# Four selective-scan layers on one core: the engines take the scans' instructions in the order of the source

## The chip, the cores and the metric

The kernel runs on one core of a Trainium2 chip. A core has a matrix engine (TensorE, PE), a vector engine (VectorE, DVE), an engine for activation functions (ScalarE, ACT), a general-purpose engine (GpSimd, POOL) and an engine that here only issues transfers (SyncE, SP). Each has its own queue of instructions and they meet through semaphores. The metric is the device time of one execution in microseconds; lower is better.

## What is computed

Four layers are applied one after the other to 8 images of 48 x 48 positions and 96 channels, each as x + layer(groupnorm(x)). A layer projects 96 channels to 2 x 192, convolves one half with a 3 x 3 window for each channel, and runs a recurrence over the 2,304 positions in four directions (by rows, by columns, and both backwards) with 16 states for each of the 192 channels. Layers 0 to 2, cut to what matters:

```python
delta = softplus(dts + bias)                    # per position and channel
def step(h, inp):
    u, dl, Bv, Cv = inp
    dA = exp(dl[..., None] * A)                 # A: 16 states per channel
    h = h * dA + (dl * u)[..., None] * Bv[:, :, None, :]
    y = einsum('bkdn,bkn->bkd', h, Cv)          # sum over the 16 states
    return (h, y)
# four directions are summed, then layernorm, times silu(z), projection to 96
```

The last layer computes h from cumulative sums in place of the recurrence; its decay makes all but the ends of the sequences vanish, and the kernel computes only those (with a full version behind a test that it makes at run time).

## The kernel before

The images go in 4 pairs; 192 channels times two images fill three tiles of 128 partitions. For each of 3 layers, 4 pairs, 3 tiles, 2 phases (rows, columns), 2 directions and 3 chunks of 768 positions there are 16 states, so 6,912 units of work. One unit, with the engine of each instruction:

```python
def pooled(self, n):                # every fourth state has dB u made on GpSimd
    return n % 4 == 3 and self.l < NLAYER - 1

def weigh(self, n):                 # POOL: bb = B (broadcast by DMA) * (delta u)
    if self.pooled(n):
        b = self.b[n][:, : self.m]
        nc.gpsimd.tensor_mul(b, b, self.du)

def exp(self, n, da):               # ACT: exp(delta A)
    ...
def spread(self, n):                # pooled: ACT puts exp(delta A) into PSUM
    ...                             # else:   PE spreads the row B over 128 partitions
    for z, zm in pieces(self.m):    #         into a PSUM tile b (two of them)
        nc.tensor.matmul(b[:, z : z + zm], w, self.brow[:k, z : z + zm], ...)

def scan(self, n):
    ...
    if not self.pooled(n):
        nc.vector.tensor_mul(b, self.du, b)                         # DVE: dB u
    h = b if self.pooled(n) else da
    nc.vector.tensor_tensor_scan(way(h), way(da), way(b), start, ALU.mult, ALU.add)
    ...
    if not self.last:
        nc.scalar.copy(carries[:, n : n + 1], h[:, end : end + 1])  # ACT: carry
    nc.gpsimd.tensor_mul(c, c, h)                                   # POOL: C h

def add_up(self, n):                # PE: sum over the states, identity matmuls
    ...
    if n == NS - 1:
        self.collect()              # DVE: y += acc
```

The loop that writes these out runs ahead for what is needed later, and weaves three generators in: `coming` (softplus of the next chunk), `behind` (the epilogue of the last pair: layernorm, gate, projection) and `ahead` (the prologue of the next pair: group norm, projections, convolution, and `split`, which cuts B and C into three bf16 parts), the last from two thirds of a pair on:

```python
LAG = 4
LOADS, DECAYS = 3, 2
...
for k, ((l, p, unit), c, n) in enumerate(todo):
    ...                             # at unit == after (2/3): ahead = begin(*following)
    get_ready(k + 1)                # loads of k + 4, spread of k + 1, weigh and exp of k + 3
    c.scan(n)
    step(coming)
    if unit >= after:
        step(ahead, 8 if l in short else 1)
    elif l in short:
        step(behind, 6)
    elif unit % 2 == 0:
        step(behind)
    if k >= LAG:
        b.add_up(n)                 # of unit k - 4
        ...
```

`short` holds the last layer. The program is written as straight code, and the compiler's scheduler decides in which order each engine takes its instructions, as long as the data allow it. Tiles come from pools with a fixed number of buffers: 9 for C (`cb`), 3 for B on GpSimd (`bb`), 5 for exp(delta A) (`da`), 2 PSUM tiles for `b`, 2 PSUM banks for everything else, 1 for the sum.

Of the kernel before, what the change touches and what calls it, by code (L numbers as in the profile page):

```python
# [35 lines left out]
BF16 = mybir.dt.bfloat16  # L39
AF = mybir.ActivationFunctionType  # L40
ALU = mybir.AluOpType

P = 128
NB, H, W, DM = 8, 48, 48, 96
# [31 lines left out]
def nx(rank):  # L76

    return 2 * rank + 4 * NS
# [17 lines left out]
def ss2d_layers_kernel(ctx: ExitStack, tc: tile.TileContext, x_in, consts, weights, out):  # L96
    nc = tc.nc
# [48 lines left out]
    for b in range(2):  # L146
# [3 lines left out]
            mybir.AxisListType.X,  # L150
            ALU.add,
        )
# [7 lines left out]
    nc.vector.tensor_reduce(  # L160
        mine, ident.rearrange("p (b q) -> p b q", b=2), mybir.AxisListType.X, ALU.add
    )
# [4 lines left out]
    class Layer:  # L167


        def __init__(self, l):  # L170
            self.l = l
            self.rank = r = RANKS[l]
            self.nx = nx(r)
            cols, n = weight_columns(r)
            wt = wpool.tile([P, n], F32, name=f"w_{l}", tag="w")
            nc.sync.dma_start(wt, weights[l])
            part = {k: wt[:, a:b] for k, (a, b) in cols.items()}
            self.inw = part["inw"][0:DM]
            self.xp = part["xp"].rearrange("p (t f m) -> p t f m", t=2, f=2)
            self.dtw = part["dtw"].rearrange("p (k d) -> p k d", k=4)  # L180
            self.outw = part["outw"].rearrange("p (t c) -> p t c", t=2)
            self.outw_2 = wpool.tile([P, 2, DM], F32, name=f"outw2_{l}", tag="outw2")
            for b in range(2):
                nc.vector.tensor_scalar_mul(
                    self.outw_2[:, b, :], self.outw[:, 1, :], mine[:, b : b + 1]
                )
            self.par = part["par"].rearrange("p (t c) -> p t c", t=2)

            self.a = wpool.tile([P, 2, 4 * NS], F32, name=f"a_{l}", tag="a")
            nc.scalar.activation(self.a, self.par[:, :, C_ALOG : C_ALOG + 4 * NS], AF.Exp)  # L190
            nc.vector.tensor_scalar_mul(self.a, self.a, -1.0)

            self.amax = wpool.tile([P, 2, 4], F32, name=f"amax_{l}", tag="amax")
            nc.vector.tensor_reduce(
                self.amax, self.a.rearrange("p t (k n) -> p t k n", n=NS),
                mybir.AxisListType.X, ALU.max,
            )
            self.dsum = wpool.tile([P, 2], F32, name=f"dsum_{l}", tag="dsum")
            nc.vector.tensor_reduce(
                self.dsum, self.par[:, :, C_D : C_D + 4], mybir.AxisListType.X, ALU.add  # L200
            )
            self.diag = None

        def make_diag(self):

            self.diag = dpool.tile([P, 2, 9, P], F32, name=f"diag_{self.l}", tag="diag")
            for t in range(2):
                for j in range(9):
                    nc.vector.tensor_scalar_mul(
                        self.diag[:, t, j, :], ident, self.par[:, t, C_CONVW + j : C_CONVW + j + 1]  # L210
                    )

        def column(self, t, c):
            return self.par[:, int(t == 2), c : c + 1]
# [22 lines left out]

    def prologue(l, p, short=False):
        ly = layers[l]
        if ly.diag is None:  # L240
            ly.make_diag()
        gn = sm2.tile([DM, 2, 2], F32, name=f"gn_{l}_{p}", tag="gn")
        xd = dram.tile([2, 2, ly.nx, L], F32, name=f"xd_{l}_{p}", tag=f"xd{ly.rank}")
        xb = dram.tile([2, 2, PARTS, 3 * NS, L], BF16, name=f"xb_{l}_{p}", tag="xb")
# [4 lines left out]
        def padded(name):  # L249
            pad = tmp.tile([P, H + 2, W + 2], F32, name=name, tag="tmp")  # L250
            nc.gpsimd.memset(pad[:, 0 : H + 2 : H + 1, :], 0.0)
            nc.gpsimd.memset(pad[:, 1 : H + 1, 0 : W + 2 : W + 1], 0.0)
            return pad
# [20 lines left out]
        def split(xt, c0, m, to):  # L274
# [13 lines left out]
                )  # L288
            yield

        pad2 = padded(f"pad2_{l}_{p}")
        for b in range(2):
            x = tmp.tile([DM, L], F32, name=f"x_{l}_{p}_{b}", tag="tmp")
# [43 lines left out]
            nc.scalar.activation(scale, scale, AF.Exp, scale=-0.5)  # L337
            nc.vector.scalar_tensor_tensor(shift, mg, -1.0, scale, ALU.mult, ALU.mult)
            yield
# [83 lines left out]
    def prepare(c):  # L423
# [16 lines left out]
        for z in range(0, c.m, HALF):  # L440
# [28 lines left out]
            yield  # L469
            nc.vector.scalar_tensor_tensor(v, v, 0.0, lg, ALU.max, ALU.add)  # L470
            yield
# [24 lines left out]
    def picked(t, n):  # L496
# [2 lines left out]
            return 2 * NR, pick2[:, n, :]  # L499
        return NR, pick[:, n : n + 1].to_broadcast([NR, P])  # L500

    class Chunk:


# [90 lines left out]
        def scan(self, n):  # L595
            m = self.m
            way = (lambda z: z) if self.d == 0 else (lambda z: z[:, ::-1])
            carries = self.group["carry"]
            start = 0.0 if self.first else carries[:, n : n + 1]
            da, c = self.da.pop(n), self.cb[n][:, :m]  # L600
            b = self.b.pop(n)[:, :m]
            if not self.pooled(n):
                nc.vector.tensor_mul(b, self.du, b)  # L603
            if self.l < NLAYER - 1:

                h = b if self.pooled(n) else da
                nc.vector.tensor_tensor_scan(way(h), way(da), way(b), start, ALU.mult, ALU.add)  # L607
            else:

                h = self.rq.pop(n)  # L610
                nc.vector.tensor_mul(b, h, b)
                nc.vector.tensor_tensor_scan(
                    way(h), ones.to_broadcast([P, m]), way(b), start, ALU.mult, ALU.add
                )
                nc.gpsimd.tensor_mul(c, c, da)
            if not self.last:
                end = m - 1 if self.d == 0 else 0
                nc.scalar.copy(carries[:, n : n + 1], h[:, end : end + 1])  # L618
            nc.gpsimd.tensor_mul(c, c, h)  # L619

        def add_up(self, n):
            if n == 0:
                self.acc = pacc.tile([P, 2 * BANK], F32, name="acc", tag="acc")
            c = self.cb.pop(n)
            for z, zm in pieces(self.m):
                nc.tensor.matmul(  # L626
                    self.acc[:, z : z + zm], ident, c[:, z : z + zm],
                    start=(n == 0), stop=(n == NS - 1),
                )
            if n == NS - 1:  # L630
                self.collect()

        def collect(self):

# [23 lines left out]
    class Edge:  # L658
# [82 lines left out]
        def add_up(self, i):  # L741
            if i == 0:
                self.acc = pacc.tile([P, 2 * BANK], F32, name="acc", tag="acc")
            c = self.cb.pop(i)
            for j in range(QUAD):
                nc.tensor.matmul(  # L746
                    self.acc[:, :EDGE], ident, c[:, j, :],
                    start=(i == j == 0), stop=(QUAD * i + j == NS - 1),
                )
            if QUAD * i + QUAD == NS:  # L750
                self.collect()

        def collect(self):
            l, p, t, s = self.l, self.p, self.t, state[self.l, self.p]
# [118 lines left out]
    def drain(g):  # L873
        for _ in g:
            pass

    def step(g, n=1):
        for _ in range(n):
            if next(g, StopIteration) is StopIteration:
                return  # L880

    groups = [(t, ph, d) for t in range(3) for ph in range(2) for d in range(2)]
    LAG = 4
    LOADS, DECAYS = 3, 2

    def run(pairs, short):
# [44 lines left out]
        drain(prepare(chunks[0]))  # L931
        coming_to = iter(chunks[1:])
        behind = ahead = coming = iter(())
        get_ready(0)
        for k, ((l, p, unit), c, n) in enumerate(todo):
            at = pairs.index((l, p))
            following = pairs[at + 1] if at + 1 < len(pairs) else None
            per = NS // QUAD if l in short else NS
            all_units = len(groups) * (per if l in short else len(SCANS) * per)

            after = 2 * all_units // 3
            if unit == after:
                drain(behind)
                if following:
                    ahead = begin(*following)
            if n == 0:
                drain(coming)
                if unit + per == all_units:
                    drain(ahead)
                coming = next(coming_to, None)  # L950
                coming = prepare(coming) if coming else iter(())
            if n == max(0, per - 1 - DECAYS):
                drain(coming)
            get_ready(k + 1)
            c.scan(n)
            step(coming)
            if unit >= after:
# [6 lines that stand above are left out]
                (bl, bp, _), b, n = todo[k - LAG]  # L964
                b.add_up(n)
                if todo[k - LAG + 1][0][:2] != (bl, bp):
                    behind = epilogue(bl, bp)
        for _, c, n in todo[-LAG:]:
            c.add_up(n)
        drain(epilogue(*pairs[-1]))  # L970

    last = NLAYER - 1
    run([(l, p) for l in range(NLAYER) for p in range(NPAIR)], (last,))


    every = sm1.tile([P, 1], F32, name="every", tag="every")
# [102 lines left out]
```

## Time and profile before

| | before |
|---|---|
| time, median of 3 runs | 25,929.62 us (25,909.55 to 25,961.06) |
| span of the profiled run | 25,950.1 us |
| mean granted TensorE clock | 0.855 of full |
| busy PE / PE loads | 20,502.7 / 9,651.0 us |
| busy DVE | 19,436.9 us |
| busy POOL | 18,407.7 us |
| busy ACT | 13,651.9 us |
| read and written | 3,650.53 and 164.07 MB, 147 GB/s |

The profile is that of one execution. "Busy" is the time in which an engine had an instruction in work[...]. A group of instructions is given as line, engine, operation, output and inputs, shapes and count, then its busy time and the mean of one, then the idle time of the engine just before them and what ended most of it. A wait is given as "engine tile line <- engine tile line", with its sum, its count and the longest. "issue" is idle time that no event of the profile explains. In the tables by stretches there are, for each engine, busy us and the number of instructions.

### The profile page before, as it was taken

To read this page: it belongs to the slowest core of one execution; us is meant where nothing else is said; L and a number is where in the kernel's file an instruction comes from. 1 tells how busy PE (TensorE), PEld (TensorE's weight loads), DVE (VectorE), ACT (ScalarE), POOL (GpSimd) and SP (SyncE) were. 2 spreads that over 40 slices of the span, in tenths; PEclk is the share of its full clock that TensorE was granted. 3 is DMA by queue.
4 is the path that set the end of the run, shared out by engine and by line. 5 is a ranking of instruction groups with operands and counts; after the bars stand their busy time and mean duration, and the time that the engine had idled before them with its cause. 6 is when DMAs were issued, how large, how long until landed. Compare 5 with 4: busy or idle time off the path is not lost. (4 is left out here: it accounts for less than half of the span.)

```text
span 25950.1 us, 229568 instructions
## 1 busy us (share of the span) xinstructions
PE 20502.7 (79%) x61890; PEld 9651.0 (37%) x61890; DVE 19436.9 (75%) x17126; ACT 13651.9 (53%) x23819; POOL 18407.7 (71%) x11561
## 2 busy tenths in 40 slices
PE   7787887887887887887887887887887887886886
PEld 2333333333433333333333433433433433334555
DVE  5867877876877877877877877877877877876443
ACT  4454554554554554554554554554554554555665
POOL 5767867867877867877877877877877877875332
PEclk8888888887888988898888897898898898897876
DMA  3545545545555555555555555545555555554121
GB/s 115 162 138 155 176 139 154 174 142 148 176 147 154 177 145 153 174 150 153 174 146 152 176 148 150 175 143 153 177 147 152 175 148 152 175 151 111 56 63 49
DMA packets 1714313, 3830.25 MB, mean 148 GB/s; under 512 B 224112, under 2 KB 588016, under 8 KB 1699824
## 3 DMA queue, kind: packets, MB, share of 16 engines
q1 hardware_dynamic: 1713008, 3815.46, 49.5%
q8 instruction: 500, 8.19, 0.1%
q14 instruction: 805, 6.59, 0.1%
HBM read 3650.53 MB, written 164.07 MB: 147 GB/s over the span
## 5 line engine op out<-in xcount | busy, mean ns | idle before, releaser
L626 PE MATMUL acc<-cb,cst 128*128 128x512 f32 (+1 forms) x27648 | 12436.5, 582 | 2350.2 <-POOL cb L619 1995.9
L619 POOL TENSOR_TENSOR cb<-cb,da 128x768 f32<-128x768 f32 x5184 | 9348.1, 1812 | 3056.7 <-DVE da L607 984.5
L626 PEld LDWEIGHTS acc<-cb,cst 128*128 128x128 f32 x27648 | 5543.0, 220 | 7898.7 <-issue 4396.8
L574 ACT ACTIVATE da<-dl,a 128x768 f32<-128x768 f32 x5184 | 4828.0, 933 | 5735.9 <-POOL cb L619 5703.7
L603 DVE TENSOR_TENSOR b<-du,b 128x768 f32<-128x768 f32 x5184 | 4871.6, 952 | 2871.6 <-PE b L591 2855.7
L607 DVE TENSOR_TENSOR_SCAN da<-da,carry,b 128x768 f32<-128x768 f32 x3456 | 6173.1, 1803 | 61.3 <-ACT da L574 3.5
L591 PE MATMUL b<-brow,pick 48*128 48x512 bf16 (+3 forms) x10368 | 2904.3, 366 | 2249.7 <-DVE da L607 1594.6
L546 POOL TENSOR_TENSOR bb<-bb,du 128x768 f32<-128x768 f32 x1728 | 3133.8, 1814 | 664.8 <-DMA bb<-xd 385.0
L619 POOL TENSOR_TENSOR cb<-cb,bb 128x768 f32<-128x768 f32 x1728 | 3135.8, 1815 | 594.8 <-issue 197.3
L607 DVE TENSOR_TENSOR_SCAN da<-da,b 128x768 f32<-128x768 f32 x1728 | 2983.4, 1743 | 28.4 <-ACT da L574 1.0
L607 DVE TENSOR_TENSOR_SCAN bb<-b,carry,bb 128x768 f32<-128x768 f32 x1152 | 2073.8, 1800 | 770.5 <-POOL bb L546 609.1
L591 PEld LDWEIGHTS <-pick 48*128 48x128 bf16 (+1 forms) x10368 | 758.7, 100 | 5014.5 <-DVE da L607 2729.1
L574 ACT ACTIVATE b<-dl,a 128x768 f32<-128x768 f32 x1728 | 1550.4, 897 | 654.5 <-DVE da L607 553.0
L618 ACT COPY carry<-da 128x1 f32<-128x1 f32 x3456 | 638.5, 185 | 2353.3 <-DVE da L607 2299.0
L262 PE MATMUL ps<-pad,diag 128*128 128x480 f32 (+1 forms) x4320 | 1801.6, 562 | 77.6 <-ACT u L227 48.2
L467 POOL TENSOR_TENSOR lg<-lg,w 128x384 f32<-128x384 f32 (+1 forms) x912 | 892.1, 978 | 1029.4 <-ACT w L465 847.5
L470 DVE SCALAR_TENSOR_TENSOR ps<-ps,lg 128x384 f32<-128x384 f32 (+1 forms) x912 | 499.8, 548 | 1127.0 <-POOL lg L468 1088.8
L607 DVE TENSOR_TENSOR_SCAN bb<-b,bb 128x768 f32<-128x768 f32 x576 | 1002.8, 1741 | 360.2 <-POOL bb L546 241.0
L262 PEld LDWEIGHTS ps<-pad,diag 128*128 128x128 f32 x4320 | 800.7, 193 | 884.6 <-issue 674.3
L450 PE MATMUL ps<-dts,w 6*128 6x384 f32 (+5 forms) x2432 | 946.6, 560 | 60.3 <-DVE ex L852 14.5
L468 POOL TENSOR_TENSOR lg<-lg,e 128x384 f32<-128x384 f32 (+1 forms) x912 | 889.9, 976 | 46.6
L791 PE MATMUL ps<-ey,cst 128*128 128x144 f32 (+1 forms) x4096 | 815.8, 345 | 120.4 <-ACT ey L815 104.0
(124 smaller groups left out, 17609.9 us busy)
## 6 DMA issues: line engine op xcount, KB each, us to landing
cb<-xd SPq DMA_DIRECT2D x4736, 384.0 KB
cb<-xd SPq DMA_DIRECT2D x4736, 192.0 KB
bb<-xd SPq DMA_DIRECT2D x1152, 384.0 KB
bb<-xd SPq DMA_DIRECT2D x1152, 192.0 KB
yd<-y SPq DMA_DIRECT2D x48, 1152.0 KB
ey<-yd SPq DMA_DIRECT2D x256, 216.0 KB
brow<-xb SPq DMA_DIRECT2D x576, 72.0 KB
xb<-parts SPq DMA_DIRECT2D x288, 108.0 KB
```

The lines of the kernel that those rows point to most:

```text
L262: nc.tensor.matmul(ps[:, :m], ly.diag[:, int(t == 2), j, :], pad[:, r0 + dy : r0 + dy + nr, dx : dx + W], start=(j == 0), stop=(j == 8),)
L450: nc.tensor.matmul(o[:, :m], ly.dtw[q0 : q0 + r, k, chans], dts[q0 : q0 + r, at], start=True, stop=True,)
L467: nc.gpsimd.tensor_sub(lg, lg, w1)
L468: nc.gpsimd.tensor_add(lg, lg, e)
L546: nc.gpsimd.tensor_mul(b, b, self.du)
L574: nc.scalar.activation(da, self.dl, AF.Exp, scale=columns_of(self.l, self.t, self.ph, self.d, n))
L591: nc.tensor.matmul(b[:, z : z + zm], w, self.brow[:k, z : z + zm], start=True, stop=True)
L603: nc.vector.tensor_mul(b, self.du, b)
L607: nc.vector.tensor_tensor_scan(way(h), way(da), way(b), start, ALU.mult, ALU.add)
L619: nc.gpsimd.tensor_mul(c, c, h)
L626: nc.tensor.matmul(self.acc[:, z : z + zm], ident, c[:, z : z + zm], start=(n == 0), stop=(n == NS - 1),)
L791: nc.tensor.matmul(o, mean_w[:, cols], z[:, b, :], start=True, stop=False)
```

## The change

The change makes each engine take the instructions of layers 0 to 2 in the order in which the source writes them. For that it draws an edge, which costs no semaphore, from every instruction to the previous one on the same engine, for the compiler's scheduler to respect. So that the written order is a fit one, it moves three things in the source: the copy of the carry and `collect` go into lists that the loop empties one unit later, just before the next scan; the product C h is written ahead of the carry copy; and the set-up of a layer (its derived weights and the diagonal matrices of the convolution) becomes steps of the prologue. Layer 3 isn't in the ordered stretch.

```diff
+    late_act, late_dve = [], []
+
+    def catch_up():
+        while late_dve:
+            late_dve.pop(0)()
+        while late_act:
+            nc.scalar.copy(*late_act.pop(0))
...
+            nc.gpsimd.tensor_mul(c, c, h)
             if not self.last:
                 end = m - 1 if self.d == 0 else 0
-                nc.scalar.copy(carries[:, n : n + 1], h[:, end : end + 1])
-            nc.gpsimd.tensor_mul(c, c, h)
+                late_act.append((carries[:, n : n + 1], h[:, end : end + 1]))
...
             if n == NS - 1:
-                self.collect()
+                late_dve.append(self.collect)
...
+    def mark():
+        marks.append(len(tc._region_blocks()[0].instructions))
+
+    def keep_order(a, b):
+        last = {}
+        info = mybir.DependencyInfo(mybir.DependencyClass.NoSync, mybir.DependencyReason.DATA)
+        for i in tc._region_blocks()[0].instructions[a:b]:
+            if i.engine in ENGINES:
+                if i.engine in last:
+                    tc.add_manual_dep(i, last[i.engine], info, reason="order")
+                last[i.engine] = i.name
...
         behind = ahead = coming = iter(())
+        mark()
         get_ready(0)
         for k, ((l, p, unit), c, n) in enumerate(todo):
...
+            if l in short and unit == 0:
+                mark()
...
             get_ready(k + 1)
+            catch_up()
             c.scan(n)
...
     run([(l, p) for l in range(NLAYER) for p in range(NPAIR)], (last,))
+
+    keep_order(*marks[:2])
```

In the layer's class (cut), what `__init__` and `make_diag` did at once becomes a generator that the prologue runs before its group norm:

```diff
+        def derive(self):
...
+            yield
...
-        def make_diag(self):
...
                     nc.vector.tensor_scalar_mul(
                         self.diag[:, t, j, :], ident, self.par[:, t, C_CONVW + j : C_CONVW + j + 1]
                     )
+                    if j % 3 == 2:
+                        yield
...
-        if ly.diag is None:
-            ly.make_diag()
...
+        if ly.diag is None:
+            for _ in range(4):
+                yield
+            yield from ly.derive()
```

More of the change, by code (lines that the diff above doesn't have):

```diff
@@ L41 @@
 ALU = mybir.AluOpType
+ENGINES = (
+    mybir.EngineType.PE, mybir.EngineType.DVE, mybir.EngineType.Activation,
+    mybir.EngineType.Pool, mybir.EngineType.SP,
+)
 P = 128
@@ L181, in __init__ @@
             self.outw = part["outw"].rearrange("p (t c) -> p t c", t=2)
+            self.par = part["par"].rearrange("p (t c) -> p t c", t=2)
+            self.diag = None
+        def derive(self):
+            l = self.l
             self.outw_2 = wpool.tile([P, 2, DM], F32, name=f"outw2_{l}", tag="outw2")
@@ L186, in __init__ @@
                 )
-            self.par = part["par"].rearrange("p (t c) -> p t c", t=2)
+            yield
             self.a = wpool.tile([P, 2, 4 * NS], F32, name=f"a_{l}", tag="a")
             nc.scalar.activation(self.a, self.par[:, :, C_ALOG : C_ALOG + 4 * NS], AF.Exp)
+            yield
             nc.vector.tensor_scalar_mul(self.a, self.a, -1.0)
@@ L201, in __init__ @@
             )
-            self.diag = None
-        def make_diag(self):
             self.diag = dpool.tile([P, 2, 9, P], F32, name=f"diag_{self.l}", tag="diag")
@@ L289, in split @@
             yield
+        if ly.diag is None:
+            for _ in range(4):
+                yield
+            yield from ly.derive()
         pad2 = padded(f"pad2_{l}_{p}")
@@ L750, in add_up @@
             if QUAD * i + QUAD == NS:
-                self.collect()
+                late_dve.append(self.collect)
         def collect(self):
@@ L880, in step @@
                 return
+    marks = []
+    def mark():
[8 more added lines that the diff above has]
+                last[i.engine] = i.name
     groups = [(t, ph, d) for t in range(3) for ph in range(2) for d in range(2)]
@@ L969, in run @@
             c.add_up(n)
+            catch_up()
         drain(epilogue(*pairs[-1]))
```

## The prediction

> **What bounds the kernel now.** I read the page first. No engine is full, and three are about equally far from it:
>
> ```profile
> PE 20502.7 (79%) x61890; PEld 9651.0 (37%) x61890; DVE 19436.9 (75%) x17126; ACT 13651.9 (53%) x23819; POOL 18407.7 (71%) x11561
> ...
> L619 POOL TENSOR_TENSOR cb<-cb,da 128x768 f32<-128x768 f32 x5184 | 9348.1, 1812 | 3056.7 <-DVE da L607 984.5
> L603 DVE TENSOR_TENSOR b<-du,b 128x768 f32<-128x768 f32 x5184 | 4871.6, 952 | 2871.6 <-PE b L591 2855.7
> L607 DVE TENSOR_TENSOR_SCAN da<-da,carry,b 128x768 f32<-128x768 f32 x3456 | 6173.1, 1803 | 61.3 <-ACT da L574 3.5
> L546 POOL TENSOR_TENSOR bb<-bb,du 128x768 f32<-128x768 f32 x1728 | 3133.8, 1814 | 664.8 <-DMA bb<-xd 385.0
> ```
>
> A unit of work here is one state of one chunk of 768 positions; layers 0 to 2 have 6,912 of them (5,184 + 1,728 scans), and DVE does one scan for each. The chain that ended last is useless here: it covers only the last 1% of the span. So I cut the span by time. The scans of layers 0 to 2 run from about 250 to 23,705 us, 1,955 us for each of 12 image pairs, and layer 3 takes the last 2,245 us. Within one pair the busy times by stretches of 100 us (columns: PE, PEld, DVE, ACT, POOL, then the granted clock, DMA share and GB/s) are very uneven:
>
> ```profile
> 10400.00:10500.00 100.00, 83.30 (x290) 40.92 (x288) 92.45 (x81) 58.80 (x102) 85.02 (x52) 0.90 0.59 183
> 11400.00:11500.00 100.00, 88.69 (x261) 40.96 (x260) 70.91 (x61) 57.16 (x83) 62.25 (x37) 0.98 0.47 135
> 11800.00:11900.00 100.00, 60.68 (x142) 26.13 (x142) 51.87 (x40) 34.39 (x55) 67.30 (x47) 0.78 0.53 141
> ```
>
> The first line is the **long part** of a pair (384 units, scans beside the epilogue of the previous pair): 10,200 to 11,200 us has 333 scans, 3.00 us per unit, with DVE 87.8% busy. The second is the convolution of the next pair's prologue, bound by PE. The third is the prologue's end (splitting B into three bf16 parts): nobody is above 70%, and 20 scans were done instead of 35. That is pure waiting. A pair is 384 x 3.00 = 1,152 us plus 803 us for the **prologue part** (192 units, 4.18 us each).
>
> The order in which the engines take their work explains much of that waiting. The timeline just at 10,000 us:
>
> ```profile
> 10001.28 1.81 POOL L619 TENSOR_TENSOR cb<-cb,bb 128x768 f32<-128x768 f32 x1 [1.35 <-issue]
> 10003.04 3.58 POOL L619 TENSOR_TENSOR cb<-cb,da 128x768 f32<-128x768 f32 x2
> ...
> 10006.57 1.82 POOL L546 TENSOR_TENSOR bb<-bb,du 128x768 f32<-128x768 f32 x1
> ...
> 10008.43 1.76 DVE L607 TENSOR_TENSOR_SCAN bb<-b,bb 128x768 f32<-128x768 f32 x1 [7.28 <-POOL bb L546]
> ...
> 10021.44 2.90 PE L626 MATMUL acc<-cb,cst 128*128 128x512 f32 x4 [3.35 <-POOL cb L619]
> ```
>
> POOL makes three products c h that nobody needs yet, while DVE stands 7.28 us for the product dB u behind them. The list of waits has these items, summed over the run:
>
> ```profile
> DVE b L603 <- PE b L591: 2855.7, 1796, 18.3
> DVE ps L470 <- POOL lg L468: 1088.8, 443, 161.6
> POOL rest L280 <- ACT parts L279: 894.5, 259, 116.1
> DVE bb L607 <- POOL bb L546: 850.1, 137, 15.1
> ```
>
> DVE's three lines are 4,795 us. Its idle time up to 23,000 us is 5,034 us (busy 17,966 us by the same table in coarser cuts), so they are nearly all of it.
>
> [...] DVE does nothing in those 7.28 us. So the order fixed at compile time is the order of execution. [...] four records of the sum over states take 1.56 us at 10,003 us and 2.90 us at 10,021 us after 3.35 us of idle (last line above), and the granted clock is 0.98 in the dense stretch and 0.78 in the loose one. [...]
>
> **The change, part by part.** It removes no arithmetic and adds none: the same scans, products and matmuls.
>
> 1. *Order.* Before, the compiler's scheduler chose each engine's sequence. Comparing the two built programs: among the 12,096 DVE instructions of the scans, 1,169 times two products stand next to each other before; after, each product is followed by its scan, in a strict round of four. On POOL, between dB u and the c h product that uses its state lie 9 to 11 other c h products in 894 of 1,728 cases and only 1 in 447 cases; after, always 3. On PE, runs of 7 to 9 sums without a spread of B vanish, and single ones rise from 2,257 to 3,413.
> 2. *Carry copies* (185 ns, 4,608 of them) come one unit later on ACT, *collect* one unit later on DVE: nothing in cost, but they no longer stand before work that is ready.
> 3. *Layer set-up* (diag and the like, 18 products of 519 ns per layer) is spread over steps: 9.3 us in each of three layers, most of it hidden already. Nothing.
>
> *Long part, per chunk of 16 units.* DVE's own work is 0.878 x 3.00 x 16 = 42.2 us. I follow the round by hand. After scan k-1, PE spreads B for unit k+1 (0.49 us for two warm matmuls) while DVE does unit k (0.95 + 1.80 = 2.75, or 1.80 where k is a GpSimd state): 1.3 us to spare at worst, so this wait goes. POOL has five products of 1.81 = 9.1 us in a round in which DVE has about 10.6 us: it keeps up. What stays: softplus's second half on POOL comes behind dB u and c h (1.81 + 1.81 + 2.0 us after scan k-1 plus 1.81 for the c h still running = 7.5 us), and DVE asks for it after two more units (2.75 x 2 = 5.5): about 2 us per chunk. With 1 to 1.5 us for the rest, 45.6 us, or **2.85 us per unit: 384 x 2.85 = 1,094 us** (now 1,152).
>
> *Prologue part, 192 units.* 45 convolution steps: PE is the bound; in the trace the spread of B comes back every 3.55 us where PE is dense (11,390.05, 11,393.60, 11,397.16): 45 x 3.6 = 162 us. 48 split steps: a chain of ACT copy 0.5, POOL 0.9, ACT 0.5, POOL 0.9 and a DMA out of a single buffer, between c h products of 1.81; I get 7 to 8 us for a pair of steps: 48 x 3.9 = 187 us. 30 projection steps at 3.3 (PE and the ACT copy): 100 us. 69 plain units at 2.85: 197 us. Sum 646, with some friction **670 us** (now 803).
>
> Per pair 1,764 instead of 1,955: -191 us, times 11.5 (the last pair's prologue is the short one): -2,200 us, 23,730. Layer 3 keeps its scheduler. I add 170 us for in-order waits that I haven't seen: **23,900 us**.
>
> **Rivals.**
> - *In-order waits replace the others, and it comes out even or slower.* With rigid order, one late item (a softplus product on POOL, a table load of 1.28 us on ACT, a PSUM bank out of two) stops everything behind it. For it: all three engines are near 80%, so there is little slack, and the 2 us per chunk above could be 5 (all that DVE gets in the long part is then lost). Against: the loop is written with leads of 2 to 4 units. It would make 25,300 to 26,500.
> - *PE becomes the bound.* The sum over states has a mean of 582 and 220 ns a record or load, a mix of warm and cold; cold, a unit needs 2.9 + 0.6 us and PE sets 3.5 us per unit: 27,000. [...]
> - *POOL becomes the bound everywhere*: 2.46 us per unit in the long part, so it can't be above 2.64 of DVE; only in the split steps. No loss there.
> - *It goes better than I think*: DVE at 97% would make 2.72 us per unit and 600 us of prologue part: 22,500.
>
> **Range and chances.** Over two thirds of the gain (133 of 191 us per pair) lies in the prologue part, where the waiting is seen plainly; the long part's share is small and uncertain. 22,900 to 25,200. Faster by over 2% means under 25,411.
>
> **What would show it.** Right: the stretches at the prologue's end have 25 to 30 scans in 100 us instead of 20 to 25; the waits of DVE for B and for dB u fall to under half; the sum's records get shorter and the mean clock rises from 0.855 to above 0.9; DVE is 80% or more busy over the span, with the same busy time. Wrong: the wait of DVE for the softplus product grows far above 1,089 us, or ACT's wait for the split's buffer does; or the long part stays at 33 scans in 100 us.

## The result and the profile after

| | before | after |
|---|---|---|
| time, median of 4 runs | 25,931.35 us | 25,154.46 us (25,140.5 to 25,180.25) |
| ratio to before, 95% interval | | 0.9701 (0.9684 to 0.9718) |
| mean granted TensorE clock of the profiled run | 0.855 | 0.876 |
| scans of layers 0 to 2 end at | 23,708 us | 22,947 us |

The order makes the kernel 777 us faster. I had predicted 2,030 us, so less than half of it came, and the time lies only just inside the upper end of the range, 25,200 us. Layer 3, which is not ordered, takes what it took (2,230 against 2,242 us). First the page of the kernel after: busy times, then the groups of the scans' instructions (busy time, mean ns of one | idle time just before them, and what ended most of it).

```profile
PE 19696.2 (78%) x61890; PEld 9459.8 (38%) x61890; DVE 19797.8 (79%) x17126; ACT 13485.8 (54%) x23806; POOL 18463.5 (73%) x11561
...
L639 POOL TENSOR_TENSOR cb<-cb,da 128x768 f32<-128x768 f32 x5184 | 9387.6, 1813 | 3692.3 <-DVE da L630 2322.7
...
L630 DVE TENSOR_TENSOR_SCAN da<-da,carry,b 128x768 f32<-128x768 f32 x3456 | 6267.5, 1814 | 244.5 <-DVE b L626 2.7
L626 DVE TENSOR_TENSOR b<-du,b 128x768 f32<-128x768 f32 x5184 | 4915.0, 948 | 826.8 <-PE b L614 822.8
...
L569 POOL TENSOR_TENSOR bb<-bb,du 128x768 f32<-128x768 f32 x1728 | 3129.4, 1811 | 23.8 <-DMA bb<-xd 16.9
```

Two columns are to be read here. The idle time before the product dB u on DVE falls from 2,871.6 to 826.8 us, and the one before POOL's dB u from 664.8 to 23.8: both as predicted. But DVE's busy time, which was to stay, rises by 361 us with the same 17,126 instructions of hardly changed means, and the idle time before the scans rises from 61.3 to 244.5 us. What else DVE waits for stands in the list of waits (sum, count, longest):

```profile
DVE ps L484 <- POOL lg L482: 1254.7, 501, 160.0
...
DVE b L626 <- PE b L614: 822.8, 624, 6.1
ACT parts L289 <- DMA xb<-parts: 789.5, 222, 9.4
...
DVE bb L630 <- ACT b L597: 716.0, 283, 10.3
...
DVE y L675 <- PE acc L649: 351.5, 176, 16.2
...
DVE y L665 <- PE acc L649: 308.6, 82, 11.1
...
DVE y L670 <- PE acc L649: 202.1, 76, 7.4
```

The first is the softplus product, now DVE's largest wait. The three lines with `y` are `collect`: 862 us for PE's sum (351.5 + 308.6 + 202.1), where there were 54 before. The wait for dB u from POOL (850.1 before) is gone. But the scans that it held, those of the GpSimd states, now wait for ACT's exponential (line `bb`), 716 us where it was 169 before: the idle time ahead of these scans falls only from 1,131 to 745 us. ACT's own wait for the split's buffer (line `parts`) has grown from 83 to 789.5 us.

Third view: the scans alone, by stretches of 100 us (busy us and number of scans, then clock, DMA share, GB/s), in the long part, the convolution and twice at the prologue's end.

```profile
10400.00:10500.00 100.00, 57.41 (x33) 0.91 0.56 171
11100.00:11200.00 100.00, 40.22 (x23) 0.95 0.40 116
11400.00:11500.00 100.00, 47.51 (x27) 0.82 0.55 152
11500.00:11600.00 100.00, 54.99 (x32) 0.83 0.61 165
```

The end of the prologue has 27 to 34 scans where it had 20 to 28; the long part still has 33. To see where a pair's time goes, I put every stretch of DVE's trace between the end of one instruction and the next start down to the instruction that waited, and took the mean over ten pairs (the second to the eleventh), in us per pair:

| units of a pair | before | predicted | after |
|---|---|---|---|
| long part, 384 | 1,164 | 1,094 | 1,167 |
| first 16 of the prologue part | 52 | 48 | 70 |
| the 48 beside the convolution | 208 | 170 | 205 |
| the last 128 | 530 | 452 | 453 |
| sum | 1,954 | 1,764 | 1,895 |

Of the column "predicted", the prediction gives only 1,094 and 670 us. The three rows of the prologue part divide its 670: 16 plain units make 46, its 45 convolution steps and 3 plain units 170, the rest 430, and its friction of 24 us is put nearly all into the last row.

So the gain is there at the prologue's end, where the waiting was seen plainly, and there is next to none elsewhere. In the long part DVE's time divides like this:

| long part, us per pair | before | after |
|---|---|---|
| DVE in work | 1,023.6 | 1,043.7 |
| idle ahead of the product (spread of B) | 81.8 | 23.0 |
| idle ahead of a scan on its own product | 2.0 | 20.3 |
| idle ahead of `collect` | 0.5 | 26.6 |
| idle ahead of softplus | 45.2 | 48.5 |

Of the 59 us that the order removes, a slower hand-over from product to scan takes 38 (20 as work, 18 as idle time) and `collect` takes 26, by this reading. The experiments test it.

### The profile page after: what moved, and what is told of

Its sections match the earlier page's. It is cut to its first block, busy times and chain, and to the rows that moved or that the text cites. A ratio compares the mean times of both kernels' runs of the same rounds, so it can differ in the third digit from the quotient of the medians.

```text
span 25177.8 us, 226429 instructions
## 1 busy us (share of the span) xinstructions
PE 19696.2 (78%) x61890; PEld 9459.8 (38%) x61890; DVE 19797.8 (79%) x17126; ACT 13485.8 (54%) x23806; POOL 18463.5 (73%) x11561
## 5 line engine op out<-in xcount | busy, mean ns | idle before, releaser
L649 PE MATMUL acc<-cb,cst 128*128 128x512 f32 (+1 forms) x27648 | 11751.8, 558 | 260.9 <-DVE y L675 69.8
L649 PEld LDWEIGHTS acc<-cb,cst 128*128 128x128 f32 x27648 | 5375.4, 211 | 6437.5 <-issue 5650.1
L630 DVE TENSOR_TENSOR_SCAN da<-da,carry,b 128x768 f32<-128x768 f32 x3456 | 6267.5, 1814 | 244.5 <-DVE b L626 2.7
L626 DVE TENSOR_TENSOR b<-du,b 128x768 f32<-128x768 f32 x5184 | 4915.0, 948 | 826.8 <-PE b L614 822.8
L597 ACT ACTIVATE da<-dl,a 128x768 f32<-128x768 f32 x5184 | 4758.9, 925 | 9.8 <-POOL cb L639 5.2
L569 POOL TENSOR_TENSOR bb<-bb,du 128x768 f32<-128x768 f32 x1728 | 3129.4, 1811 | 23.8 <-DMA bb<-xd 16.9
L468 ACT ACTIVATE ps<-ps,w 128x384 f32<-128x384 f32 (+1 forms) x912 | 491.8, 539 | 1334.0 <-PE ps L464 1330.4
```

The source lines that it names most:

```text
L597: nc.scalar.activation(da, self.dl, AF.Exp, scale=columns_of(self.l, self.t, self.ph, self.d, n))
L649: nc.tensor.matmul(self.acc[:, z : z + zm], ident, c[:, z : z + zm], start=(n == 0), stop=(n == NS - 1),)
```

## Experiments

In the ratios all runs are compared with the kernel before (25,902 to 25,923 us in these comparisons); "gain on the change" is against 25,154 us. The theory at the start: the written order alone makes the gain, and most of the expected rest is eaten by DVE's own product-to-scan dependence and by hand-overs that come with too little lead (`collect`, softplus, the split's buffers). Rivals: the moved carry and collect are what gains; DVE's extra time is no matter of dependence; PE is the bound.

| run | median, us | ratio (95%) | on the change, us |
|---|---|---|---|
| no_order | 25,943.05 | 1.0012 (1.0004 to 1.0020) | +789 |
| order_not_late | 25,712.9 | 0.9930 (0.9913 to 0.9946) | +558 |
| collect_after_scan | 24,934.36 | 0.9625 (0.9609 to 0.9641) | -220 |
| no_dependence (leaves delta u out of the recurrence) | 24,802.84 | 0.9567 (0.9551 to 0.9583) | -352 |
| softplus_later | 24,500.47 | 0.9456 (0.9440 to 0.9471) | -654 |
| two_part_buffers | 24,923.99 | 0.9621 (0.9601 to 0.9640) | -230 |
| products_in_pairs | 25,222.46 | 0.9733 (0.9717 to 0.9750) | +68 |
| three_together | 23,839.8 | 0.9194 (0.9177 to 0.9210) | -1,315 |
| products_ahead | 29,636.29 | 1.1442 (1.1423 to 1.1461) | +4,482 |
| prologue_spread | 25,283.38 | 0.9764 (0.9747 to 0.9780) | +129 |
| third_of_taps (leaves work out) | 24,511.26 | 0.9466 (0.9451 to 0.9482) | -643 |
| three_and_pairs | 24,590.38 | 0.9497 (0.9482 to 0.9513) | -564 |

**1. The change without its edges.**

```diff
-    keep_order(*marks[:2])
```

> The changed kernel without the edges: the carry copy and the collect still come one unit later in the source, but the scheduler chooses each engine's order again. If the order is what gains (my theory), this is level with the kernel before, 25,700 to 26,000 us, and DVE's wait for the spread of B is back at 2,500 us or more. If the moved carry and collect are what gains (rival), it is level with the changed kernel, 25,150 us.

It took the time of before. The list of waits of this run has both old waits at their old size:

```profile
DVE b L626 <- PE b L614: 2820.2, 1811, 12.4
...
DVE bb L630 <- POOL bb L569: 891.6, 159, 15.1
```

So the moved carry, collect and set-up gain nothing while the scheduler chooses; the edges do.

**2. The edges, with carry and collect at their old places.**

```diff
-                late_act.append((carries[:, n : n + 1], h[:, end : end + 1]))
+                nc.scalar.copy(carries[:, n : n + 1], h[:, end : end + 1])
...
-                late_dve.append(self.collect)
+                self.collect()
```

> The edges alone: carry copy and collect stand where the kernel before had them, directly behind the scan and behind the last sum. If the later place matters under a fixed order, this is slower than the changed kernel by 1 to 3% (25,400 to 25,900 us), because ACT's carry copy then holds back the next exponentials and DVE's collect comes right after PE has begun the last sum; DVE's wait at the collect rises above 862 us. If it doesn't matter: 25,150 us within 0.5%.

The time is in the expected range, the reason only half: `collect` waits no longer than in the change (340 and 288 us in its two largest items). What grows is ACT's wait for the scan before it can copy the carry, 5,646 us against 1,823 in the change:

```profile
ACT carry L642 <- DVE da L630: 5646.4, 2459, 6.6
```

ACT then stands with everything behind the copy, and hands it on: DVE waits 523 us for ACT ahead of its products delta u, against 117 in the change. These 406 us are most of the difference in time. Under a fixed order, moving the two by one unit is worth 558 us; without it, nothing (run 1). The edges alone gain 196 us. The order and the leads belong together.

**3. `collect` after the scan instead of ahead of it.**

```diff
-        while late_dve:
-            late_dve.pop(0)()
+    def catch_up_dve():
+        while late_dve:
+            late_dve.pop(0)()
...
             c.scan(n)
+            catch_up_dve()
```

> The changed kernel with the collect written behind the next scan instead of ahead of it. In the changed kernel DVE waits 862 us in all for PE's last sum at the collect. Theory: this wait is a real loss and a scan in its place fills it: DVE's wait at the collect falls under 200 us and the time to about 24,500 to 24,700 us. Rival: PE's first sum of the next chunk needs the single PSUM tile that the collect frees, so the wait only moves to PE and comes back at the spread of B: within 0.5% of 25,150 us.

`collect`'s wait falls from 862 to about 60 us, but the wait for the spread of B rises from 823 to 1,204 and the softplus wait from 1,255 to 1,349: of some 800 us, 220 are kept, less than the theory's 450 or more and more than the rival allows. Here a wait that is removed partly comes back at the next late producer.

**4. The product of DVE goes to a tile that nobody reads**, and the scan takes the spread B itself. This leaves the factor delta u out of the recurrence for three states of four; the same instructions of the same shapes run in the same order.

```diff
+            elif not self.pooled(n):
+                nobody = bbpool.tile([P, SCAN], F32, name="nobody", tag="nobody")
+                nc.vector.tensor_mul(nobody[:, :m], self.du, b)
```

> Leaves out the use of the product: in layers 0 to 2 DVE writes delta u B into a tile that nobody reads, and the scan reads B as it was spread, so the result is another; the instructions, their shapes and their order are the same, only the scan doesn't depend on the product just ahead of it. In the changed kernel a scan starts 1.01 us after its product does, where independent neighbours start 0.85 us after. Theory: strict product, scan, product, scan costs 0.13 to 0.15 us in each of 5,184 units, so this falls by 550 to 780 us, to about 24,400 to 24,600 us, and the start-to-start time to 0.86 us. Rival: the gap is filled by waits on other engines anyway, and the time stays within 0.7% of 25,150 us.

This is the disputed cost by itself. The timeline of DVE in the change (start, duration), product and then its scan:

```profile
10310.40 0.95 DVE L626 TENSOR_TENSOR b<-du,b 128x768 f32<-128x768 f32 x1
10311.46 1.81 DVE L630 TENSOR_TENSOR_SCAN da<-da,carry,b 128x768 f32<-128x768 f32 x1
```

The same in this run:

```profile
10300.46 0.93 DVE L629 TENSOR_TENSOR nobody<-du,b 128x768 f32<-128x768 f32 x1
10301.30 1.81 DVE L633 TENSOR_TENSOR_SCAN da<-da,carry,b 128x768 f32<-128x768 f32 x1
```

From start to start it is 1.06 us there and 0.84 here. The medians over all such pairs are 1.014 us with the dependence and 0.846 without; two independent products next to each other in the kernel before are 0.850 apart. The independent successor above starts 0.09 us before the record of the first has ended (10,301.30 and 10,301.39), the dependent one 0.11 us after it (10,311.46 and 10,311.35): overlap counts once, and that is why "busy" grew by 361 us with nearly the same means. It is not the product's new place in SBUF either: in run 7, where all products stay in PSUM, a scan starts 0.865 us after another state's product and 1.045 after its own. And the order makes such neighbours: 1,159 of the 5,184 products are followed directly by their own scan before, 5,178 after. As an estimate, 4,019 more at 0.168 us, two thirds of them in the long part of 12 pairs, make 38 us per pair there, as much as the table shows. The scans' group of this run has no idle time at all ahead of it (last column):

```profile
L633 DVE TENSOR_TENSOR_SCAN da<-da,carry,b 128x768 f32<-128x768 f32 x3456 | 6248.7, 1808 | 0.0
```

In the long part work falls from 1,043.7 to 1,015.2 us per pair and the idle time ahead of scans from 20.3 to 0, while softplus (48.5 to 58.7) and the GpSimd states (5.5 to 10.6) take some of it. In the whole 352 us go with the dependence, less than the 550 to 780 expected.

**5. Softplus's second half on DVE one step later.**

```diff
             nc.gpsimd.tensor_add(lg, lg, e)
             yield
+            yield
```

> The changed kernel with one more unit between GpSimd's two softplus operations and DVE's use of them. In the changed kernel DVE waits 1,255 us there, 48.5 us of it in the long part of each pair. Theory: with a fixed order DVE must be given as much lead over GpSimd as GpSimd is late; one more unit (2.8 us) covers nearly all of it: the wait falls under 400 us and the time to 24,400 to 24,700 us. Rival: the wait was GpSimd's only chance to catch up, and comes back at other places where DVE meets it or at the exponentials: within 0.7% of 25,150 us.

The largest single gain, from one line, as the theory had it. Its wait in the list:

```profile
DVE ps L485 <- POOL lg L482: 390.9, 56, 159.5
```

Of 501 waits 56 are left; in the long part the item falls from 48.5 us per pair to 0. A step is one unit, 3.0 us of lead in the long part.

**6. Two buffers for the parts of B and C.**

```diff
-            parts = sm1.tile([ly.nx, PARTS, SCAN // 2], BF16, name="parts", tag="parts")
-            rest = sm1.tile([ly.nx, SCAN // 2], F32, name="rest", tag="rest")
+            parts = sm2.tile([ly.nx, PARTS, SCAN // 2], BF16, name="parts", tag="parts")
+            rest = sm2.tile([ly.nx, SCAN // 2], F32, name="rest", tag="rest")
```

> The changed kernel with two buffers in place of one for the bf16 parts and the rest of the split. ACT waits 790 us for the transfer out of the single buffer, and behind it the exponentials for the GpSimd states come late (DVE waits 39 us per pair for them at the end of the prologue). Theory: this wait holds the split stretch, so its 391 us per pair (units 464 to 575) fall to about 365, and the time by 250 to 350 us to 24,800 to 24,900 us. Rival: GpSimd's work sets the split stretch (it is 85% busy there): within 0.4% of 25,150 us.

ACT's wait for the transfer out of `parts` (789.5 us) is gone, and another, which had 244.5 us in the change, takes half of its place:

```profile
ACT parts L292 <- POOL rest L290: 632.3, 241, 4.5
```

The end of the prologue (units 464 to 575) falls from 391.3 to 377.3 us per pair, half of what the theory expected, and DVE's wait for ACT's exponentials from 716 to 580 us.

**7. Products in pairs**: product 0, product 1, scan 0, scan 1, product 2, scan 2, scan 3, so that fewer scans follow their own product.

```diff
+            elif n % 4 == 0:
+                self.product(n)
+                self.product(n + 1)
+            elif n % 4 == 2:
+                self.product(n)
```

> The changed kernel with the order product 0, product 1, scan 0, scan 1, product 2, scan 2, scan 3 in each round of four, so that only one of the three scans stands directly behind its own product; same results. Theory: a dependent neighbour costs DVE 0.15 us, so DVE's busy time and gaps fall by two thirds of what the run without the dependence took off (352 us): about -230 us, 24,900 to 24,950 us. Rival: product 1 now asks for the spread of B only 0.85 us after the scan that frees its PSUM tile, in place of 2.8 us, so DVE's wait for the spread rises above 823 us by more than is gained: 25,200 to 25,600 us.

DVE saves what the theory says (in the long part work 1,043.7 to 1,026.0, idle ahead of scans 20.3 to 8.6), and the whole is 68 us slower: the second product asks PE for its spread one scan earlier, and that wait goes from 823 to 1,215 us. The rival was right: what DVE saves, it then waits for PE.

```profile
DVE b L620 <- PE b L614: 1214.8, 809, 8.8
```

**8. Runs 3, 5 and 6 together.**

> Collect behind the scan, softplus one unit later and two buffers for the split, together. If the three waits are independent, the gains add up: -220 us (measured for the first), -600 and -300 us (expected for the others), about 24,050 us. If each wait only hides another engine's lag (GpSimd is near 82% busy, PE near 80%), they don't add up: 24,500 to 24,800 us.

At 23,839.8 us this is the fastest version that computes everything. The single gains add up to 1,104 us; together they give 1,315, more than either expectation had. The long part falls to 1,089.5 us per pair. Its page, and its largest wait on DVE:

```profile
PE 19124.1 (80%) x61890; PEld 9260.2 (39%) x61890; DVE 19757.2 (83%) x17126; ACT 13526.7 (57%) x23806; POOL 18437.2 (77%) x11561
```

```profile
DVE b L629 <- PE b L617: 1290.1, 915, 8.0
```

The mean clock of its profiled run is 0.899. DVE's largest wait is now that for PE's spread; softplus, the largest in the change, has 438 us left.

**9. The product one unit ahead, into SBUF.** If the dependence costs time, a product made a unit earlier should save it; here it goes into an SBUF tile of its own.

```diff
+    bupool = ctx.enter_context(tc.tile_pool(name="bu", bufs=3))
...
+            self.b[n] = o = bupool.tile([P, SCAN], F32, name="bu", tag="bu")
+            nc.vector.tensor_mul(o[:, : self.m], self.du, b)
```

> The changed kernel with DVE's product written to an SBUF tile of its own and one unit ahead of the scan that reads it (order: product 0, scan 3, scan 0, product 1, product 2, scan 1, scan 2); same results. The PSUM tile of the spread is then free right after the product. Theory: two waits go, that of the scan for its own product (352 us in the run without the dependence) and most of DVE's 823 us for the spread of B: about 24,300 to 24,500 us. Rival: the scan now reads both operands from SBUF, beside GpSimd, and if the two get in each other's way, scans or GpSimd's products take longer than 1.81 us and the time is 24,900 us or more.

The rival of that expectation came true, far beyond its size. The dependence is gone (0.0 idle ahead of the scans), but scan and product both got longer. Groups of the page:

```profile
L647 POOL TENSOR_TENSOR cb<-cb,da 128x768 f32<-128x768 f32 x5184 | 12668.3, 2459 | 1475.2 <-DVE da L638 820.2
...
L638 DVE TENSOR_TENSOR_SCAN da<-da,carry,bu 128x768 f32<-128x768 f32 x3456 | 9408.3, 2735 | 0.0
```

In the change the scan reads one operand from PSUM and takes 1.81 us; with both in SBUF its mean is 2.735, and GpSimd's product goes from 1.813 to 2.459. The timelines of POOL and of DVE show each of them lengthened beside the other:

```profile
10005.01 1.81 POOL L647 TENSOR_TENSOR cb<-cb,da 128x768 f32<-128x768 f32 x1
...
10012.30 3.12 POOL L647 TENSOR_TENSOR cb<-cb,bb 128x768 f32<-128x768 f32 x1 [1.91 <-PE b L615]
```

```profile
10005.56 2.87 DVE L638 TENSOR_TENSOR_SCAN da<-da,bu 128x768 f32<-128x768 f32 x1
...
10012.08 1.73 DVE L638 TENSOR_TENSOR_SCAN da<-da,bu 128x768 f32<-128x768 f32 x1
```

The first scan starts while POOL's product runs and ends 1.61 us after that product's end (10,008.43 and 10,006.82). The second scan starts first and takes 1.73; now POOL's product, begun 0.22 us after it, ends 1.61 us after the scan's end. In both cases it is as if the one that starts second ran only after the first; what holds it, no run shows. Over the whole trace, the scans of this kind that start while POOL is at work have a mean of 2.93 us (4,134 of them), those that start with POOL idle 1.81; in the change the same two groups have 1.79 and 1.79. A fifth combination, this one with 10 and with the other three (five_together: 29,468.08 us, ratio 1.1383, 1.1364 to 1.1402), has the same collision (scans 2.706, GpSimd's products 2.420 us), and its other parts can't be read.

> All of it: collect behind the scan, softplus one unit later, two buffers for the bf16 parts, products one unit ahead (two tiles), prologue begun earlier and thinner. Three of them gave 23,840 us. If the other two add up: 22,700 to 23,000 us. If PE or GpSimd takes over as the bound by then (both near 18,500 to 19,700 us busy): 23,200 to 23,500 us.

**10. The prologue from 7/12 of a pair on, in three units of four.**

```diff
-            after = 2 * all_units // 3
+            after = (2 * all_units // 3) if l in short else (7 * all_units // 12)
...
-                step(ahead, 8 if l in short else 1)
+                step(ahead, 8 if l in short else int(unit % 4 > 0))
```

> The changed kernel with the prologue begun at 7/12 of a pair in place of 2/3 and stepped in three of four units: 45 convolution steps, at 3.95 us of PE time a unit, fall on 60 units. In the changed kernel the convolution stretch is PE-bound (units 384 to 463 take 337 us, 4.2 us a unit) while the units ahead of it have neither prologue nor epilogue. Theory: thinner PE work costs less, 20 to 35 us per pair: 24,750 to 24,900 us. Rival: the work is only moved: within 0.4% of 25,150 us.

1,904 us per pair against 1,895, and 129 us slower in the whole, a little outside the rival's range too: thinning it out only moved the work.

**11. Three of the convolution's nine taps**, which leaves out two thirds of the convolution's matmuls.

```diff
+                    if j % 3 == 0:
...
-                            stop=(j == 8),
+                            stop=(j == 6),
```

> The changed kernel with three of the nine taps of the convolution: six of nine matmuls are left out, so the result is another, and nothing else changes. Theory: PE sets the convolution stretch (units 400 to 447 of a pair take 205 us, 4.28 us a unit, as they did before the change, with PE up to 99% busy); with 0.8 us in place of 2.4 us a step the stretch falls to DVE's pace with its other waits, 145 to 155 us, 50 to 60 us per pair, and the whole, with the convolutions of the first prologue and of layer 3 that nothing covers, to 24,200 to 24,500 us. Rival: the stretch is held by the order of the steps (ACT waiting for the matmuls, PSUM banks) and falls by less than 25 us per pair: 24,650 us or more.

The 48 units beside the convolution fall from 205 to 173 us per pair, between what the two theories expected. DVE's wait for the spread, over the run, is halved:

```profile
DVE b L627 <- PE b L615: 409.9, 314, 6.2
```

By the division of DVE's trace, its waits for PE in these units (for the spread, and for the sum at `collect`) fall from 51 to 19 us per pair. So the six taps account for 32 of the 59 us that these units take above those of the long part (48 x 3.04 = 146 us). What the three remaining taps cost was not measured.

**12. Three together, with the products in pairs.** Once the other hand-overs have their leads, the pairs might show their saving.

> Collect behind the scan, softplus one unit later, two buffers for the split (23,840 us together), and the products in pairs. On the changed kernel the pairs took off 17.7 us of DVE work and 11.7 us of gaps per pair in the long part, and lost them to longer waits for the spread (+14), for softplus (+8) and at the collect (+3). Theory: the softplus and collect waits are gone here, so only the spread's is left to grow, and 10 to 17 us per pair stay: 23,640 to 23,720 us. Rival: PE, which now has 0.85 us for the spread of product 1, is at its limit and takes it all back: 23,800 to 24,000 us.

They don't: it is 750 us slower than three_together, far beyond the rival's range. The dependence is saved again (24 us per pair), and the wait for PE's spread doubles; why it grows so much more than in run 7 is not shown:

```profile
DVE b L623 <- PE b L617: 2643.4, 1664, 7.9
```

## Why the prediction was wrong in size

- **The order itself: right.** The waits for B and for POOL's dB u fell to under half, and the edges do it (run 1). The traces keep the order of the built programs: among the scans' instructions on DVE two products follow each other 1,169 times in the trace before, as often as the prediction counts in the program, and never in the trace after. But a good part of the second came back as a wait for ACT at the same scans, which I had not foreseen. And "nobody needs yet" was too strong: PE had waited 1.59 us for the first of the three products c h and took each within 0.1 us of its end. It was DVE that did not need them.
- **The prologue's end: right, to the microsecond by luck.** 453 us against 452 for its last 128 units, with 27 to 34 scans in 100 us. DVE's idle time there falls from 186 to 111 us per pair: ahead of the product from 94 to 8 and for dB u from 67 to nothing, as expected, but 42 for ACT's exponential are new, and `collect` rises from 2 to 22 and softplus from 10 to 24.
- **"DVE's own work is ... 42.2 us" per chunk: the term that failed first.** I took it from the kernel before, "with the same busy time". The base was a little short: the 333 scans count those on the edge of two stretches twice, there are 329, so 3.04 us per unit and 1,164 us for the long part before, not 1,152. And the order itself changes it: before, 1,159 products had their own scan directly behind them, after, 5,178. Work and idle time ahead of scans are 44.3 us per chunk (1,043.7 + 20.3, by 24), 51 us per pair above the 42.2, and run 4 puts the dependence at 352 us of the whole. The first sign was in the prediction's own step 1, which counts the 1,169 neighbouring products, and I gave them no cost.
- **"About 2 us per chunk" for softplus: right**, 48.5 us for 24 chunks, 2.02 each. I left it as a cost; run 5 shows that one line removes it.
- **"1 to 1.5 us for the rest": 2.3.** `collect` is 1.1 of it, which I had called "nothing in cost"; the spread of B is 0.96, where I wrote "this wait goes"; the rest is 0.2. Run 3 shows that 220 us can be had back at `collect`. With the term above this makes the long part 1,167 and not 1,094 us, none of its gain: 73 of the 131 us that a pair missed.
- **"45 convolution steps ... at 3.6": too short.** I had read 3.55 us at a narrow chunk. The timeline of PE after, in a full one:

```profile
11127.63 0.49 PE L614 MATMUL b<-brow,pick 96*128 96x512 bf16 x2
11127.96 2.58 PE L272 MATMUL ps<-pad,diag 128*128 128x480 f32 x6
11130.38 1.45 PE L649 MATMUL acc<-cb,cst 128*128 128x512 f32 x4
11131.67 0.49 PE L614 MATMUL b<-brow,pick 96*128 96x512 bf16 x2
```

  The spread comes back after 4.04 us, with 2.58 us of it for a unit's part of the convolution at 480 columns. Four of five pieces of the convolution have 480 columns, so PE sets 3.94 us a step (an estimate from 4.04 and 3.55), and the 48 units would take 186. They took 4.28 us each, 205, which is 35 us per pair more than I gave them. In them DVE waits 19 us at `collect` for PE's sum, where I had no cost; run 11 shows PE as the cause of 32 us, and the rest stays open.
- **The first 16 units, 70 against 48 us**: 22 per pair. Against the kernel before (52) DVE has 8 us more of work, most of it group norm and set-up, which I had put at "nothing" and which now stand in these units, and 11 us more of idle time: 4.5 at `collect`, 3.5 ahead of the group norm's first instructions, which wait for their loads in line ahead of scans. No run tested this.
- **"Mean clock ... above 0.9", "DVE is 80% or more busy": both missed**, 0.876 and 79%. With the rest of the leads (run 8) they are 0.899 and 83%. The sum's records did get shorter, from 582 to 558 ns. That the sum took 2.90 us at 10,021 us "after 3.35 us of idle" was misread: the granted clock is 0.50 from 10,016.90 us on, and PE's spread at 10,017.27 us, ahead of that idle time, already takes 0.82 us in place of 0.49. What halved the clock, no run shows.
- **The rival "in-order waits replace the others"** was stronger than its weight: in the long part, where all of the expected gain was lost, though not in the whole. It named softplus for this, which stayed at 2 us per chunk; what won was the hand-over on DVE and `collect`. A sign of being wrong came true, the long part staying at 33 scans in 100 us, and ACT's wait for the split's buffer, which the prediction names as another, grew from 83 to 789.5 us.

Run 8 shows that the 23,900 us could be had from this order, with a lead for `collect` and softplus and a second buffer for the split that the change doesn't give.

## What to carry to other kernels

A fixed order needs leads: with the carry copy and `collect` at their old places it gained 196 us here. Where the order is fixed, an instruction that takes something from another engine should stand as far behind its producer as the producer can be late, and here two such moves and a second buffer were worth more than the whole change (1,315 against 777 us). An order also changes an engine's own time (DVE's by 361 us here), so "same instructions, same busy time" has to be looked at, by the distance from start to start of the neighbours that it creates. What one engine gains by asking earlier, another must be able to give: pairing the products saved DVE time and lost it at PE (the wait for the spread went from 823 to 1,215 us).

## What the runs showed of the hardware

- A DVE product of 128 x 768 float32 and what follows it are 0.85 us apart from start to start if the second does not need the first (0.850 to a second product in the kernel before, 0.846 to the scan in run 4), and 1.01 us to its own scan (1.014 in the change). Between this product and its scan the dependence costs 0.17 us.
- A scan with both operands in SBUF beside GpSimd's products, which read SBUF: a mean of 2.735 instead of 1.81 us, the products 2.459 instead of 1.813, the kernel 29,636 instead of 25,154 us (run 9). In the change, where the scan has one operand in PSUM, it takes 1.79 us beside a busy POOL and 1.79 beside an idle one.
